# Graph stack of four layers: feature sums in column groups, spreads as one float32r pass, the diagonal as a row of the last row tile

## The chip, the cores and the metric

The kernel runs on one core of a Trainium2 chip. The metric is the device time of one execution in microseconds (us). Before the change the median of 14 runs is 944.88 us, from 942.43 to 948.26. Engines are called PE (TensorE, with PEld for its weight loads), DVE (VectorE), ACT (ScalarE), POOL (GpSimd) and SP (SyncE, which issues most DMAs).

## What is computed

The input is a feature matrix x of 2708 nodes by 128 features and a sparse, non-negative adjacency of 2708 x 2708, all float32. Four layers follow one another, each as x = layernorm(x + layer(x, adj)) without learned scale: graph convolution, an attention by degrees, a hyperbolic layer and a layer with node and edge weights. The last two and the norms, cut to what matters here:

```python
def _layernorm(x, axis=-1, eps=1e-5):
    m = jnp.mean(x, axis=axis, keepdims=True)
    v = jnp.var(x, axis=axis, keepdims=True)
    return (x - m) / jnp.sqrt(v + eps)

# layer 1: attention
H = A @ (att @ XW)
# layer 2: hyperbolic
h = proj(mobius_add(proj(mobius_matvec(weight, x)), proj(expmap0(bias))))
support_t = adj @ logmap0(h)
h = proj(expmap0(support_t))          # needs the norm of every node's row
xt = relu(logmap0(h))
h = proj(expmap0(xt))                 # and the norm after relu
# layer 3: node and edge
node_output = concat((adj > 0) @ x, (adj < 0) @ x) @ node_weight + node_bias * diag(adj)[:, None]
edge_output = (adj @ x) @ edge_weight + edge_bias * diag(adj)[:, None]
out = node_output + edge_output + x
```

## The kernel before

Nodes are cut into NT = 22 tiles of 128 rows (the last has 20) and into NB = 6 column blocks of 512 nodes (the last has 148). From the attention's end on, activations lie feature-major: 128 features on the partitions, the block's nodes along the free side. All of the change but its constants lies in `fast_rest` (from L1458), which runs from about 504 us to the end, in three stages of six blocks each.

*Attention stage.* `product(weights, b)` (L1486) sums 22 f32 matmuls over the adjacency's row tiles, taken from `pieces` (L1770), which loads two halves of a column block per call through SP (L1784, and L1789 for the 20-row tile). `after_attention(b)` (L1531) adds the old x (L1538), squares (L227), gets the variance of every node by `feature_sums` (L1502: per tile of 128 nodes one matmul with the squares as weights and one output column, so node-major), takes sqrt and reciprocal (L1541, L1542), spreads the result over the features with four transposes (`spread`, L241), multiplies (L1544) and makes `mx` (L1548). After blocks 2, 4 and 5 `hyperbolic` (L1562) works on the tiles so far, on DVE and ACT alone, and writes the h tiles (L1570).

*Hyperbolic stage.* The same product on h. `after_hyperbolic(b)` (L1646) needs two norms per node: sums of the squares of the product (usq) and of its relu (rsq), both by `column_sums_at` (su, L1502); then on 128 x 8 elements sqrt, reciprocal and Tanh (L1657 to L1664), a spread (pg), the residual (L1669), a mean by a 512-column matmul with a matrix of 1/128 (L1671), its subtraction (L1672), and `norm_wide` (L245): square, a 512-column matmul for the variance (L248), sqrt and reciprocal on 128 x 512 (L249, L250), and the multiply. The products with the last layer's weights (pp, L1677) give `edge` (L1685) and `node` as two float32r terms (L1688, L1689).

*Last stage.* For every row tile k there is an f32 matmul with `edge` (L1715) and two float32r ones of `node` with a 0/1 mask of the adjacency (L1704, L1724). Where k lies in the block, the diagonal comes in: `dg` is the adjacency tile times the identity on DVE (L1735), and a matmul with `bsum`, the sum of both biases in every row, adds it (L1736). Then the residual (L1745), `norm_wide` and the store (L1748).

A float32 matmul shows in the profile as two MATMUL records, a float32r one as one. PSUM work tiles come from `scratch()`, which goes round three tags and four buffers. The engines' instruction orders are set when the program is built, by a scheduler with pins in the source (`issue_after`, `queued`), and each engine runs its own in turn. Column groups of the PE array, where a matmul's output lies on 32 of the PSUM partitions or on one row at 0, 32, 64 or 96, occur once before: `whole_sum` (L758), for four row sums of the first attention steps.

## Time and profile before

| | us |
|---|---|
| median of 14 runs | 944.88 |
| the profiled execution | 945.75 |
| its span, first to last instruction | 944.0 |
| PE busy in the span | 883.2 |
| DVE busy | 538.6 |
| ACT busy | 368.2 |
| attention stage | 515 to 632 |
| hyperbolic stage | 654 to 763 (its product begins at 626) |
| last stage | 763 to 944 |
| mean granted PE clock | 0.965 |

The stages were read from the timeline of PE. A page's group row gives the line, the engine, output and inputs by name, the shapes and the count; after the bar come the busy time and the mean ns of one, then the idle time of the engine ahead of it and what released it. In the timeline a row starts with start and length in us, and brackets give the idle time ahead and the releaser. In a row by windows each engine's busy time stands with its number of instructions, then the granted clock, the DMA share and GB/s.

### The profile page before, as it was taken

To read this page: it belongs to the slowest core of one execution; us is meant where nothing else is said; L and a number is where in the kernel's file an instruction comes from. 1 tells how busy PE (TensorE), PEld (TensorE's weight loads), DVE (VectorE), ACT (ScalarE), POOL (GpSimd) and SP (SyncE) were. 2 spreads that over 40 slices of the span, in tenths; PEclk is the share of its full clock that TensorE was granted. 3 is DMA by queue.
4 is the path that set the end of the run, shared out by engine and by line. 5 is a ranking of instruction groups with operands and counts; after the bars stand their busy time and mean duration, and the time that the engine had idled before them with its cause. 6 is when DMAs were issued, how large, how long until landed. Compare 5 with 4: busy or idle time off the path is not lost.

```text
span 944.0 us, 9050 instructions
## 1 busy us (share of the span) xinstructions
PE 883.2 (94%) x3166; PEld 459.2 (49%) x3166; DVE 538.6 (57%) x1097; ACT 368.2 (39%) x595; POOL 149.0 (16%) x169
## 2 busy tenths in 40 slices
PE   3799999789799999999999999989999999999997
PEld 2344555435344444444444444454454555555555
DVE  4785557898588888887784004354423363444233
ACT  3776331210777776666663113355222221000000
POOL 5211000302765553222110000000000000000000
PEclk9799999797899999999999999999999999999998
DMA  9996930195596445334423677387664374555410
GB/s 342 369 317 231 301 120 23 50 386 201 189 351 213 148 154 168 118 123 143 148 88 121 242 262 267 118 322 271 236 228 156 100 291 163 197 180 200 148 44 15
DMA packets 93077, 182.81 MB, mean 194 GB/s; under 512 B 3680, under 2 KB 20784, under 8 KB 92896
## 3 DMA queue, kind: packets, MB, share of 16 engines
q1 hardware_dynamic: 82832, 142.35, 42.7%
q0 software_dynamic: 8320, 37.76, 12.1%
q10 hardware_dynamic: 1872, 2.04, 0.6%
q8 instruction: 27, 0.44, 0.2%
q14 instruction: 26, 0.21, 0.1%
HBM read 179.31 MB, written 2.83 MB: 193 GB/s over the span
## 4 chain that ended last, share of the span: by engine, by line
PE 80%; DVE 12%; DMA 4%; ACT 2%; issue 2%; ACTq 0%; DVEq 0%
PE a L1486 21%; PE uacc L1401 13%; PE a L1715 11%; PE a L821 10%; PE num L1436 7%; PE a L1724 6%; DVE att L1449 4%; DMA A<-in_adjT_dram 4%; PE t L758 2%; DVE jk L1203 2%; DVE att L1430 2%; PE var L248 1%; PE pp L1677 1%; PE su L1502 1%; PE low L1268 1%
## 5 line engine op out<-in xcount | busy, mean ns | idle before, releaser
L1401 PE MATMUL uacc<-att,xw_g 128*128 128x512 f32 (+1 forms) x312 | 130.4, 554 | 9.0 <-DVE att L1449 8.2
L1441 ACT ACTIVATE ln<-num,inval,occ_l 128x512 f32<-128x512 f32 (+1 forms) x156 | 106.5, 722 | 65.2 <-DVE gat L1440 62.8
L1715 PE MATMUL a<-cb,ut 128*128 128x512 f32 (+2 forms) x264 | 124.9, 555 | 0.0
L1724 PE MATMUL a<-mask,node 128*128 128x512 f32 (+2 forms) x264 | 123.0, 546 | 0.0
L1436 PE MATMUL num<-gat,w_all 128*128 128x512 f32 (+1 forms) x276 | 114.1, 543 | 0.0
L1486 PE MATMUL a<-cb,q_b 128*128 128x512 f32 (+2 forms) x264 | 108.4, 552 | 0.0
L821 PE MATMUL a<-A,q_b 128*128 128x512 f32 (+2 forms) x264 | 106.8, 552 | 0.7 <-DMA A<-in_adjT_dram 0.7
L1486 PE MATMUL a<-cb,xw 128*128 128x512 f32 (+2 forms) x264 | 106.1, 547 | 0.0
L1401 PEld LDWEIGHTS uacc<-att,xw_g 128*128 128x128 f32 x312 | 55.9, 189 | 90.7 <-issue 50.0
L1392 POOL DMA_INDIRECT gat<-in_adjT_dram,row_i x52 | 76.2, 1466 | 145.0 <-PE num L1436 77.4
L1440 DVE COPY gat<-num 2x512 f32<-2x512 f32 x150 | 85.8, 608 | 2.2 <-PE num L1436 2.0
L1449 DVE TENSOR_TENSOR att<-att,ln 128x1354 f32<-128x1354 f32 x52 | 81.1, 1560 | 9.8 <-ACT ln L1448 9.6
L1724 PEld LDWEIGHTS a<-mask,node 128*128 128x128 f32 (+1 forms) x264 | 49.0, 192 | 51.3 <-issue 50.7
L247 ACT ACTIVATE wsq<-s 128x512 f32<-128x512 f32 (+1 forms) x12 | 7.0, 581 | 169.8 <-DVE s L1745 137.0
L1436 PEld LDWEIGHTS num<-gat,w_all 128*128 128x128 f32 x276 | 51.2, 191 | 41.4 <-issue 22.7
L821 PEld LDWEIGHTS a<-A,q_b 128*128 128x128 f32 (+1 forms) x264 | 46.0, 191 | 50.3 <-issue 47.5
L1448 ACT ACTIVATE ln<-ln 128x1354 f32<-128x1354 f32 x52 | 69.4, 1334 | 1.3
L1430 DVE TENSOR_SCALAR att<-q_b,gj_l 128x1354 f32<-128x1354 f32 x52 | 48.0, 926 | 37.8 <-PE uacc L1401 37.8
L1486 PEld LDWEIGHTS a<-cb,q_b 128*128 128x128 f32 (+1 forms) x264 | 46.0, 191 | 48.1 <-issue 46.5
L1486 PEld LDWEIGHTS a<-cb,xw 128*128 128x128 f32 (+1 forms) x264 | 45.4, 190 | 47.2 <-issue 47.2
L1704 DVE TENSOR_SCALAR mask<-cb 128x3072 fp32r<-128x3072 f32 (+5 forms) x24 | 33.4, 1393 | 49.9 <-PE a L1724 49.9
L1036 ACT ACTIVATE xw<-A 128x2048 f32<-128x2048 f32 (+3 forms) x36 | 57.0, 1583 | 7.7 <-DMA A<-in_adjT_dram 6.8
(410 smaller groups left out, 937.5 us busy)
## 6 DMA issues: line engine op xcount, KB each, us to landing
cb<-in_adjT_dram SPq DMA_DIRECT2D x15, 2816.0 KB
cb<-in_adjT_dram SPq DMA_DIRECT2D x15, 2560.0 KB
A<-in_adjT_dram SPq DMA_DIRECT2D x25, 1024.0 KB
B<-in_adjT_dram SPq DMA_DIRECT2D x18, 1024.0 KB
cb<-in_adjT_dram SPq DMA_DIRECT2D x3, 814.0 KB
cb<-in_adjT_dram SPq DMA_DIRECT2D x3, 740.0 KB
ut<-in_adjT_dram SPq DMA_DIRECT2D x2, 1024.0 KB
A<-in_adjT_dram SPq DMA_DIRECT2D x5, 296.0 KB
```

The source lines that it names most:

```text
L821: nc.tensor.matmul(acc[c][:, :w], lhsT=z[:kw, k, :], rhs=t[:kw, i, :w], start=c not in begun, stop=(d == NB - 1 and k == NT - 1), skip_gro ...
L1392: return nc.gpsimd.indirect_dma_start(out=gat[g], out_offset=None, in_=adj_h, in_offset=bass.IndirectOffsetOnAxis(ap=row_i[:, h, g : g + 1 ...
L1401: nc.tensor.matmul(uacc[c][:, : cb - ca], lhsT=xw_g[:, g, :], rhs=att[:, ca:cb], start=(g == 0), stop=(g == GM - 1),)
L1430: nc.vector.tensor_scalar(att, q_b[:, h0 : h0 + HALF], gj_l[:, g : g + 1], 1.0, op0=ALU.mult, op1=ALU.max)
L1436: nc.tensor.matmul(num[:, : cb - ca], lhsT=(w_first if g < FIRST else w_all)[:, g, :], rhs=gat[g][:, ca:cb], start=True, stop=True)
L1440: nc.vector.tensor_copy(gat[g + 1][0:2, ca:cb], num[0:2, : cb - ca])
L1441: nc.scalar.activation(ln_n[:, ca:cb], num[:, : cb - ca], AF.Ln, scale=occ_l[:, g : g + 1], bias=inval[:, g : g + 1],)
L1448: nc.scalar.activation(ln_n, ln_n, AF.Exp, scale=-1.0)
L1449: nc.vector.tensor_mul(att, att, ln_n)
L1486: nc.tensor.matmul(acc[:, :w], lhsT=weights[:kw, k, :], rhs=pc[:kw, t, :w], start=(k == 0), stop=(k == NT - 1),)
L1715: nc.tensor.matmul(acc[:, :w], lhsT=edge[:kw, k, :], rhs=pc[:kw, t, :w], start=(k == 0), stop=False, skip_group_check=True,)
L1724: nc.tensor.matmul(acc[:, :w], lhsT=node[:kw, k, j, :], rhs=mask[:kw, t - ma, :w], start=False, stop=(k == NT - 1 and j == 1), skip_group_ ...
```

## The change

*Constants.* `sel` (128 x 4, float32r, made on POOL) has ones in rows 32i and 32i + 1 of column i. `odd` is 1 on odd partitions and `sign` 1 on even, -1 on odd ones (two DVE operations in `prepare_rest`).

*Feature sums.* `group_sums` takes the constant (ones or 1/128) as weights, 32 columns of it, and the squares of one tile of 128 nodes as the moving side; tile i's result goes to PSUM partitions 32i to 32i + 31. The sums of a block thus lie on four groups of partitions, 128 nodes along the free side. `group_spread` brings a value back over all features: ACT multiplies by `sign` and rounds to float32r, DVE adds the rest on the odd partitions, so even and odd rows add up to the value; then one float32r matmul per tile with a column of `sel` broadcast as weights. `group_roots` and `norm_groups` do sqrt, reciprocal and norm on 128 x 128 instead of 128 x 512.

*Where they are used.* Attention: blocks 0 to 4; the variances also go back to node-major by a matmul of 128 x 4 (`v4` with `ident[:, ::32]`), since `hyperbolic` needs them so. Block 5 keeps its form, but PE's order there is pinned: two, two and two row tiles of the next product stand before its st, pr and mx matmuls (`meanwhile`). Hyperbolic: all six blocks, with the mean as a third group sum of s and no mean matmul after the residual; the mean is subtracted ahead of the product with g. Last stage: blocks 0 to 4; block 5 keeps `norm_wide`.

*The diagonal.* `dg` and its matmuls go. The last row tile has 20 rows; its second-half piece gets the adjacency's diagonal of the block as row 20 (1 x 512, from `diag_d` in DRAM, through SP), and `edge` gets `bsum` as its row 20 (a DMA on POOL between the stages), so that the L1715 matmul of k = 21 adds the biases. `diag_d` is filled by one DMA of 2708 single elements on SP, right after `prepare_rest` and ahead of the loads of the attention's B tiles.

```diff
     nc.gpsimd.tensor_scalar(pad_big, pad_big, 1.0e30, None, op0=ALU.mult)
+    sel = const.tile([P, 4], F32R, tag="sel", name="sel")
+    sel_f = const.tile([P, 4], F32, tag="sel_f", name="sel_f")
+    nc.gpsimd.memset(sel_f, 0.0)
+    for i in range(4):
+        nc.gpsimd.memset(sel_f[32 * i : 32 * i + 2, i : i + 1], 1.0)
+    nc.gpsimd.tensor_copy(sel, sel_f)
+    odd = const.tile([P, 1], F32, tag="odd", name="odd")
+    sign = const.tile([P, 1], F32, tag="sign", name="sign")
     neg_sum = const.tile([P, NB * NB], F32, tag="neg_sum", name="neg_sum")
...
         nc.vector.tensor_add(bsum, b3n_s, b3e_s)
+        nc.vector.tensor_reduce(odd, ident.rearrange("p (a b) -> p b a", b=2)[:, 1, :], AX.X, ALU.add)
+        nc.vector.tensor_scalar(sign, odd, -2.0, 1.0, op0=ALU.mult, op1=ALU.add)
         centre(w3_s.rearrange("p (n f) -> p n f", f=F), 3, "w3_m")
...
     xw_d = tc.dram_tile([NP, F], F32, name="xw_d")
+    diag_d = tc.dram_tile([N, 1], F32, name="diag_d")
     w_col = w1ext[:, F : F + 1]
...
             prepare_rest()
+        nc.sync.dma_start(out=diag_d, in_=bass.AP(tensor=adjT.tensor, offset=0, ap=[[N + 1, N], [1, 1]]))
...
         rot = {"n": 0}
+        latest.clear()
...
-        def product(weights, b, name):
+        begun = {}
+        def product(weights, b, name, upto=NT, fixed=False):
             w = width(b)
-            acc = psum.tile([P, BW], F32, tag=f"acc{b % 3}", name=name)
-            for i in range(2):
-                pc = pieces(b, i)
-                for t in range(KH):
-                    k = i * KH + t
-                    kw = rows(k)
+            if name not in begun:
+                begun[name] = [psum.tile([P, BW], F32, tag=f"acc{b % 3}", name=name), 0, None]
+            acc, done, pc = begun[name]
+            for k in range(done, upto):
+                i, t = divmod(k, KH)
+                if t == 0:
+                    pc = pieces(b, i)
+                kw = rows(k)
+                with queued(PE) if fixed else nullcontext():
                     nc.tensor.matmul(
...
                     )
+            begun[name] = [acc, upto, pc]
             return acc
+        def meanwhile(b, n):
+            if b == NB - 1:
+                product(h, 0, "a2_0", n, True)
+                return queued(PE)
+            return nullcontext()
...
                 )
+        def group_sums(st, at, sq, b, w_cols):
+            for i in range(len(tiles(b))):
+                nc.tensor.matmul(
+                    st[32 * i : 32 * i + 32, at : at + P],
+                    lhsT=w_cols[:, :32],
+                    rhs=sq[:, i * P : (i + 1) * P],
+                    start=True,
+                    stop=True,
+                )
+        def group_spread(name, r, b):
+            n = len(tiles(b))
+            two = blk.tile([P, P], F32R, tag="two", name=f"two_{name}", bufs=3)
+            nc.scalar.activation(two[: 32 * n, :], r, AF.Copy, scale=sign[: 32 * n, :])
+            nc.vector.scalar_tensor_tensor(
+                two[: 32 * n, :], r, odd[: 32 * n, :], two[: 32 * n, :].bitcast(F32), op0=ALU.mult, op1=ALU.add
+            )
+            ps = scratch(name)
+            for i in range(n):
+                nc.tensor.matmul(
+                    ps[:, i * P : (i + 1) * P],
+                    lhsT=sel[: 32 * n, i : i + 1].to_broadcast([32 * n, P]),
+                    rhs=two[: 32 * n, :],
+                    start=True,
+                    stop=True,
+                )
+            return ps
+        def group_roots(name, st, b):
+            n = 32 * len(tiles(b))
+            r = blk.tile([P, P], F32, tag="gr", name=name)
+            nc.scalar.activation(r[:n, :], st[:n, :P], AF.Sqrt, bias=eps_c[:n, :])
+            nc.vector.reciprocal(r[:n, :], r[:n, :])
+            return r[:n, :]
+        def norm_groups(q, s, b, out):
+            st = scratch(f"st_{q}{b}")
+            group_sums(st, 0, square_block(s, b, f"sq_{q}{b}"), b, mean_w)
+            pr = group_spread(f"pr_{q}{b}", group_roots(f"gr_{q}{b}", st, b), b)
+            nc.vector.tensor_mul(out, s, pr[:, : width(b)])
...
             nc.vector.tensor_add(s[:, :w], acc[:, :w], x[:, cs])
-            st = feature_sums(square_block(s[:, :w], b, f"asq{b}"), b, f"st1_{b}", mean_w[:, 0:1])
+            asq = square_block(s[:, :w], b, f"asq{b}")
+            if b == NB - 1:
+                with meanwhile(b, 2):
+                    st = feature_sums(asq, b, f"st1_{b}", mean_w[:, 0:1])
+            else:
+                sg = scratch(f"sg{b}")
+                group_sums(sg, 0, asq, b, mean_w)
+                v4 = blk.tile([P, P], F32, tag="v4", name=f"v4_{b}")
+                nc.vector.tensor_copy(v4, sg[:, :P])
+                pr = group_spread(f"pr{b}", group_roots(f"gr{b}", sg, b), b)
+                st = scratch(f"st1_{b}")
+                nc.tensor.matmul(st[:, :4], lhsT=v4, rhs=ident[:, ::32], start=True, stop=True)
             nc.vector.tensor_copy(var[:, ta:tb], st[:, :n])
...
             nc.vector.reciprocal(rstd[:, ta:tb], rstd[:, ta:tb])
-            pr = spread(scratch(f"pr{b}"), rstd[:, ta:tb], b)
+            if b == NB - 1:
+                with meanwhile(b, 4):
+                    pr = spread(scratch(f"pr{b}"), rstd[:, ta:tb], b)
             nc.vector.tensor_mul(x[:, cs], s[:, :w], pr[:, :w])
...
                 pm = scratch(f"mx{t0}")
-                for i in range(2):
-                    nc.tensor.matmul(
-                        pm[:, i * (F + 1) : (i + 1) * (F + 1)],
-                        lhsT=x[:, (t0 + i) * P : (t0 + i + 1) * P],
-                        rhs=w2ext,
-                        start=True,
-                        stop=True,
-                    )
+                with meanwhile(b, 6):
+                    for i in range(2):
+                        nc.tensor.matmul(
+                            pm[:, i * (F + 1) : (i + 1) * (F + 1)],
+                            lhsT=x[:, (t0 + i) * P : (t0 + i + 1) * P],
+                            rhs=w2ext,
+                            start=True,
+                            stop=True,
+                        )
                 pv = pm[:, : 2 * (F + 1)].rearrange("p (t f) -> p t f", f=F + 1)
...
             s = blk.tile([P, BW], F32, tag="s", name=f"s2_{b}")
+            if w % P:
+                nc.gpsimd.memset(s[:, w : n * P], 0.0)
             su = scratch(f"su{b}")
-            column_sums_at(su, square_block(acc[:, :w], b, f"usq{b}"), b, ones[:, 0:1])
+            group_sums(su, 0, square_block(acc[:, :w], b, f"usq{b}"), b, ones)
             nc.vector.tensor_scalar(s[:, :w], acc[:, :w], 0.0, None, op0=ALU.max)
-            column_sums_at(su, square_block(s[:, :w], b, f"rsq{b}"), b, ones[:, 0:1], at=n)
-            nr = small("unr", 8)
-            inv = small("uinv", 8)
-            nc.vector.tensor_scalar(nr[:, : 2 * n], su[:, : 2 * n], MIN_NORM2, None, op0=ALU.max)
-            nc.scalar.activation(nr[:, : 2 * n], nr[:, : 2 * n], AF.Sqrt)
-            nc.vector.reciprocal(inv[:, : 2 * n], nr[:, : 2 * n])
-            g = small("g", 4)
-            nc.vector.tensor_scalar(g[:, :n], inv[:, :n], ATANH_MAX, 1.0, op0=ALU.mult, op1=ALU.min)
-            nc.vector.tensor_mul(g[:, :n], g[:, :n], nr[:, n : 2 * n])
-            nc.scalar.activation(g[:, :n], g[:, :n], AF.Tanh)
-            nc.vector.scalar_tensor_tensor(
-                g[:, :n], g[:, :n], MAXNORM, inv[:, n : 2 * n], op0=ALU.min, op1=ALU.mult
-            )
-            pg = spread(scratch(f"pg{b}"), g, b)
+            group_sums(su, 2 * P, s, b, mean_w)
+            group_sums(su, P, square_block(s[:, :w], b, f"rsq{b}"), b, ones)
+            pm = group_spread(f"mean{b}", su[: 32 * n, 2 * P : 3 * P], b)
+            nr = blk.tile([P, 2 * P], F32, tag="unr", name=f"unr{b}", bufs=1)[: 32 * n]
+            inv = blk.tile([P, 2 * P], F32, tag="uinv", name=f"uinv{b}", bufs=1)[: 32 * n]
+            g = blk.tile([P, P], F32, tag="ug", name=f"ug{b}", bufs=1)[: 32 * n]
+            nc.vector.tensor_scalar(nr, su[: 32 * n, : 2 * P], MIN_NORM2, None, op0=ALU.max)
+            nc.scalar.activation(nr, nr, AF.Sqrt)
+            nc.vector.reciprocal(inv, nr)
+            nc.vector.tensor_scalar(g, inv[:, :P], ATANH_MAX, 1.0, op0=ALU.mult, op1=ALU.min)
+            nc.vector.tensor_mul(g, g, nr[:, P:])
+            nc.scalar.activation(g, g, AF.Tanh)
+            nc.vector.scalar_tensor_tensor(g, g, MAXNORM, inv[:, P:], op0=ALU.min, op1=ALU.mult)
+            nc.vector.tensor_sub(s[:, :w], s[:, :w], pm[:, :w])
+            pg = group_spread(f"pg{b}", g, b)
             nc.vector.tensor_mul(s[:, :w], s[:, :w], pg[:, :w])
             nc.vector.tensor_add(s[:, :w], s[:, :w], x[:, cs])
-            pm = scratch(f"mean{b}")
-            nc.tensor.matmul(pm[:, :w], lhsT=mean_w, rhs=s[:, :w], start=True, stop=True)
-            nc.vector.tensor_sub(s[:, :w], s[:, :w], pm[:, :w])
-            norm_wide(scratch(f"var2_{b}"), s[:, :w], b, x[:, cs], blk.tile([P, BW], F32, tag="sq", name=f"wsq2_{b}"), blk.tile([P, BW], F32, tag="rs", name=f"rs2_{b}"))
+            norm_groups("l2_", s[:, :w], b, x[:, cs])
             for t0 in range(ta, tb, 2):
...
+        kw = rows(NT - 1)
+        nc.gpsimd.dma_start(out=edge[kw : kw + 1, NT - 1, :], in_=bsum[0:1, :])
...
             for i in range(2):
-                pc = pieces(b, i)
+                pc = pieces(b, i, i == 1)
                 for ma, mb in ((0, 6), (6, KH)):
...
                         kw = rows(k)
+                        ke = kw + (k == NT - 1)
                         nc.tensor.matmul(
                             acc[:, :w],
-                            lhsT=edge[:kw, k, :],
-                            rhs=pc[:kw, t, :w],
+                            lhsT=edge[:ke, k, :],
+                            rhs=pc[:ke, t, :w],
                             start=(k == 0),
...
                             )
-                        if k in tiles(b):
-                            o = k * P - b * BW
-                            dg = blk.tile([P, P], F32, tag="dg", name=f"dg{k}")
-                            nc.vector.tensor_mul(dg[:kw, :kw], pc[:kw, t, o : o + kw], ident[:kw, :kw])
-                            nc.tensor.matmul(
-                                acc[:, o : o + kw],
-                                lhsT=bsum[:kw, :],
-                                rhs=dg[:kw, :kw],
-                                start=False,
-                                stop=False,
-                                skip_group_check=True,
-                            )
             s = blk.tile([P, BW], F32, tag="s", name=f"s3_{b}")
...
             ob = blk.tile([P, BW], F32, tag="ob", name=f"ob{b}")
-            norm_wide(scratch(f"var3_{b}"), s[:, :w], b, ob[:, :w], blk.tile([P, BW], F32, tag="sq", name=f"wsq3_{b}"), blk.tile([P, BW], F32, tag="rs", name=f"rs3_{b}"))
+            if b == NB - 1:
+                norm_wide(scratch(f"var3_{b}"), s[:, :w], b, ob[:, :w], blk.tile([P, BW], F32, tag="sq", name=f"wsq3_{b}"), blk.tile([P, BW], F32, tag="rs", name=f"rs3_{b}"))
+            else:
+                norm_groups("l3_", s[:, :w], b, ob[:, :w])
             nc.sync.dma_start(out=outT[:, cs], in_=ob[:, :w])
...
-                def pieces(b, i):
+                def pieces(b, i, diagonal=False):
...
                     if i:
-                        nc.sync.dma_start(out=t[: rows(NT - 1), full, :w], in_=adjT[k0 + full * P :, cs])
+                        kw = rows(NT - 1)
+                        nc.sync.dma_start(out=t[:kw, full, :w], in_=adjT[k0 + full * P :, cs])
+                        if diagonal:
+                            nc.sync.dma_start(
+                                out=t[kw : kw + 1, full, :w], in_=diag_d[cs, :].rearrange("c o -> o c")
+                            )
                     return t
```

## The prediction

> **What bounds the kernel now.** I read the page from the top: busy shares, then the chain.
>
> ```profile
> span 944.0 us, 9050 instructions
> PE 883.2 (94%) x3166; PEld 459.2 (49%) x3166; DVE 538.6 (57%) x1097; ACT 368.2 (39%) x595; POOL 149.0 (16%) x169
> PE 80%; DVE 12%; DMA 4%; ACT 2%; issue 2%; ACTq 0%; DVEq 0%
> ```
>
> TensorE sets the end. The change lies in the three stages after 515 us, so I cut there (PE busy is the first figure after the length):
>
> ```profile
> 515.00:632.00 117.00, 114.22 (x369) 57.53 (x368) 30.13 (x152) 32.08 (x92) 0.19 (x1) 0.99 0.67 237
> 654.00:763.00 109.00, 106.88 (x357) 56.14 (x356) 38.58 (x62) 32.09 (x55) 0.19 (x1) 0.99 0.58 207
> 763.00:924.00 161.00, 161.00 (x520) 92.56 (x519) 64.07 (x76) 11.81 (x22) 0.21 (x1) 0.99 0.45 161
> ```
>
> PE never stops inside a stage. A PE pass added or removed there moves the end by its cadence, and DVE and ACT matter only where PE waits: at the two seams. The timeline of PE around them:
>
> ```profile
> 625.37 0.61 PE L1502 MATMUL st<-mean_w,asq 128*128 128x1 f32 x4 [0.96 <-ACT asq L227]
> 628.76 0.66 PE L241 MATMUL pr<-ident,rstd 128*128 128x128 f32 x2 [1.81 <-DVE rstd L1542]
> 758.49 1.13 PE L1671 MATMUL mean<-s,mean_w 128*128 128x512 f32 x2 [0.55 <-DVE s L1669]
> 761.12 1.99 PE L248 MATMUL var<-wsq,mean_w 128*128 128x512 f32 x2 [1.50 <-ACT wsq L247]
> ```
>
> Last, the groups that the change touches (window 500 to 944 us):
>
> ```profile
> L248 PE MATMUL var<-wsq,mean_w 128*128 128x512 f32 x20 | 12.4, 706 | 2.0 <-ACT wsq L247 1.9
> L1736 PE MATMUL a<-dg,bsum 128*128 128x128 f32 x42 | 8.1, 273 | 0.0
> L1671 PE MATMUL mean<-s,mean_w 128*128 128x512 f32 x10 | 5.5, 627 | 0.6 <-DVE s L1669 0.6
> L1502 PE MATMUL su<-ones,rsq 128*128 128x1 f32 x44 | 5.4, 242 | 0.0
> L241 PE MATMUL pg<-ident,g 128*128 128x128 f32 x22 | 3.4, 273 | 0.0
> ```
>
> These durations overlap, so I price by cadence (start to start). Two records make one f32 matmul: 512 columns cost 0.86 us, 0.92 with what stands around a lone one; four feature sums 0.79 to 0.85; a spread of four transposes 0.43 (0.108 each); an L1736 product 0.22 (a k step of the last stage takes 1.54 with it, 1.32 without).
>
> **The Trainium skill.** "TensorEngine Tiling (Array Packing)", Tiling Modes, says that tiles of the array work in parallel and that changing the mode drains the engine. The trace agrees: `whole_sum` (L758) already uses four column groups; at 196.28 its four 512-column f32 matmuls start 7 ns apart and end within 0.86 us, where in turn they would take 3.4. Entering the mode leaves 0.10 us, leaving it 0.15 to 0.2: 0.3 a visit. "TensorE: Matmul & The Clock Gate", Part 1, says that idle time lowers the clock; here, after the wait before 628.76, 512-column passes take 0.85 us instead of 0.43 for about two passes. "DMA: Bandwidth & Descriptors", on the semaphore increment of 16, lets a hardware-issued DMA use the largest k up to 16 that divides the outer dimension: 2708 = 4 x 677 gives 4 engines and 677 descriptors each. No transfer of before shows that count.
>
> **The change part by part.** One visit of `group_sums` (four 128-column f32 matmuls side by side) is 0.21 (a quarter of 0.86) plus 0.30 = 0.51; bounds 0.21 and, run in turn, 0.86 + 0.30. A spread by four one-pass f32r matmuls is shown nowhere. The L1724 f32r passes cost 0.23 at 512 columns, so 0.06 each if only streaming counts, 0.19 if each waits for its weight load (192 ns on the page). I take the transposes' 0.108, so 0.43; bounds 0.24 and 0.76.
>
> *Attention, five blocks:* sums 0.79 become 0.51; a 128 x 4 matmul on `ident` that brings the variances back to node-major adds 0.21; spread alike. −0.07 each, −0.4 in all. The q_b writes (0.61 us for two at L1570) come ahead of block 3's x: +0.5.
>
> *Hyperbolic, five blocks:* before: su 1.62, pg 0.43, mean 0.93, var 0.91 = 3.89. After: one visit for usq 0.51, a double one for s and rsq 0.72, one for the norm 0.51, three spreads 1.29 = 3.03. −0.86 each, −4.3; the short block 5 pays its mode changes, +0.5. Between su and pg now lie a 128 x 256 reciprocal (1.75 by 6.3 ns a column; 0.20 before), ACT and DVE steps and a table load (1.28): 6.3 to 6.9 us, under 7.3 to 8.2 us of PE work queued between. Hidden with 1.0 to 1.5 to spare in blocks 0 to 3; without that cover up to 0.5 a block.
>
> *Last stage:* 22 L1736 products go, −4.8; five var products go, −4.55; five visits plus spreads come, +4.7. Their st and pr waits beside mask work on DVE +0.4. Total −4.2. The DVE multiplies for L1736 also go, worth nothing (DVE 40% busy). Block 5's norm keeps its form, so the tail from 937.5 to 944 stays.
>
> *Seam attention to hyperbolic:* waits and slow clock cost 4.1 before (1.1 + 2.0 + 1.0). PE's order there is now written out: two k steps of the next product before st_5, two more before pr_5, two more before mx_5. But on ACT block 5's sqrt stands behind block 4's Ln and Tanh and their table loads (1.28 each); before, it came ahead of Tanh. Adding up: its reciprocal ends 8.5 us after the product's end, PE reaches pr_5 after 4.0. A wait of 4.6 plus 2.3 of slow clock, about 7: +3 (bounds 0 and +4). What is late next: x, mx_5 and the h tiles 20 and 21, needed about 30 us after the product's end and ready at 29. It takes part of the 0.5 margin that h had (ready 649.5, read 649.9).
>
> *Seam hyperbolic to last:* 4.6 before. After: no mean wait of 0.55, no var wait of 1.5 with its clock; instead pg waits 1.7 (chain 6.3 against 4.6 of PE work, no next product behind it), and the first mask on DVE holds up a spread by 0.6; 0.7 for mode changes and clock. 3.0: −1.5 (bounds −3 and +1).
>
> *DMAs.* The diagonal goes to `diag_d` on SP behind the A loads, ahead of the B loads (first B issue 99.7 us). At 9 ns of engine time a packet (what 8-byte packets on the ACT queue show) it takes 677 x 9 ns = 6 us; at the 86 ns apart that those show between 2-KB packets, 58. The B tiles land by 126 and are first used at 178.6 (L758): 52 us of cover, the DMA nearly idle from 126 on. I take it as hidden; at 58 it would cost about 6. On SP its issue stands ahead of the twenty B issues, which need nothing from it but their turn. The six 1 x 512 row loads follow 2.8-MB loads on the same queue, issued a block ahead; only the next load stands behind them. POOL has nothing else to do after 500 us, and its `edge` row has 28 us until k = 21 of block 0. I put all of these at nothing under that cover.
>
> Sum: −0.4 + 0.5 − 4.3 + 0.5 − 4.2 + 3 − 1.5 = −6.4. The profiled run took 945.75 against a median of 944.88, so it is 0.9 above; the difference is applied to the median: 938.5. (1.75 of it lie outside the span, and I leave them as they are.)
>
> **The rivals.**
> *A, more than summed:* a mode change costs 0.1 instead of 0.3 a visit, and the written k steps cover half of what the first seam gains: about 25 visits x −0.2 = −5, and −1.5, so −12.9: 932. For it: L758's 7 ns; against it: the drains seen beside it.
> *B, the seam eats it:* pr_5's wait drags mx_5 past the h tiles' use; 5 to 6 instead of 3, and hyperbolic pg waits in blocks 0 to 3 cost 0.5 each: 942.5. For it: Ln and Tanh ahead in ACT's order; against: h still arrives within a microsecond of its use.
> *C, slower: f32r spreads bound by their weight loads.* Each of about 106 new f32r matmuls then costs 0.19 to 0.22 instead of 0.108, +0.08 to 0.11 each, +9 to +12: 949. It decides from 0.17 us a matmul on, where 106 x 0.06 eats the 6.4. For it: the LDWEIGHTS of 192 ns stand beside every f32r pass, and here no 0.43 us f32 pass hides them. Against: the transposes have loads of the same 128 columns (0.12 to 0.14 each) and keep 0.108.
> *D, slower too: diagonal descriptors at 90 ns or more*, 61 us, 9 beyond the cover; the B loads wait behind it on the same engines, and L758 at 178.6 for them: 938.5 + 9 = 947.5, and more if slower still.
> *E, no change in effect:* column groups in turn, 0.64 x 25 visits = +16, is excluded by L758 unless 128-column passes behave otherwise; I give it 0.02 within C's side.
>
> **How the numbers follow.** Main case 0.50 (934.5 to 941.5), A 0.14, B 0.16, C with E 0.12, D 0.08. Predicted: 938.5. Range: A's 931 to 947: C and D's 0.2 lies mostly above, their milder half within. The measurement tells about 0.2%, 1.9 us, from no change: faster takes the main case, A and half of B, 0.50 + 0.14 + 0.08 = 0.72; same takes the other half of B: 0.08; slower C and D, 0.20.
>
> **What the profile of the changed kernel would show.** L1736 gone and k steps of the last stage all 1.32 apart. The four matmuls of `group_sums` starting within 20 ns, with 0.1 us ahead of them and 0.2 behind. The four f32r matmuls of a spread 0.43 us from first to last end; 0.7 or more means C. PE waiting some 4 to 5 us ahead of pr_5, released by DVE's rstd. After the hyperbolic stage one wait near 1.7 on DVE's or ACT's part of `two_pg`, and none for mean or var. Windows before 515 us unchanged; a wait of L758 on a B tile means D. Wrong altogether if PE shows idle time inside a stage, which before had none.

## The result and the profile after

The changed kernel takes 939.56 us (median of 10 runs, 936.55 to 941.62) beside 944.59 for the one before: 0.9947 of it, 95% interval 0.9935 to 0.9958. A second measurement of the same kernel, beside the last experiments, gave 0.9955 (0.9940 to 0.9971). So it is some 5 us faster; 938.5 was forecast. The sum is right to about 1.4 us, but two of its terms, those of the seams, were wrong by more, with opposite signs.

The page after begins:

```profile
span 935.7 us, 9403 instructions
PE 871.7 (93%) x3290; PEld 447.0 (48%) x3290; DVE 536.8 (57%) x1115; ACT 380.5 (41%) x629; POOL 150.1 (16%) x178
```

The span fell by 8.3 us, more than the medians. That is chance ahead of the change: the first product of the attention stage starts at 508.77 us before and at 504.73 after, on code that is the same but for the diagonal's load and the constants. Over all traces of this study that start lies between 504.7 and 511.4 (509.51 in a second trace of the very same changed kernel), with PE's clock low in different places. From that start on, the stages of one program repeat closely: 430.96 and 430.84 us in the two traces of the changed kernel, 435.26 before. So I compare traces from there. "Slow clock" and "slow passes" below mean stretches in which the profile shows PE's granted clock at half.

The windows of both kernels, cut at the same points of the program (the end of the attention products, of block 1's and block 4's hyperbolic product, of blocks 1, 4 and 5 of the last stage; each row gives the length, the busy time of PE, PEld, DVE, ACT and POOL, PE's granted clock, the DMA share, GB/s). Before:

```profile
515.20:624.10 108.90, 108.90 (x352) 54.41 (x351) 24.76 (x115) 27.03 (x84) 0.19 (x1) 1.00 0.64 226
624.10:672.00 47.90, 45.12 (x124) 21.01 (x123) 26.89 (x158) 23.81 (x44) 0.00 (x0) 0.96 0.81 294
672.00:749.10 77.10, 77.04 (x237) 38.87 (x236) 26.26 (x41) 21.63 (x40) 0.00 (x0) 1.00 0.48 165
749.10:828.60 79.50, 77.45 (x287) 47.51 (x286) 33.47 (x49) 12.87 (x24) 0.40 (x2) 0.98 0.59 213
828.60:922.40 93.80, 93.80 (x296) 53.11 (x295) 35.42 (x36) 3.96 (x6) 0.00 (x0) 1.00 0.41 144
922.40:937.10 14.70, 14.31 (x93) 12.39 (x92) 6.16 (x7) 1.32 (x2) 0.00 (x0) 0.88 0.05 19
```

After:

```profile
511.00:619.00 108.00, 108.00 (x364) 52.18 (x362) 30.74 (x127) 29.05 (x87) 0.19 (x1) 1.00 0.65 228
619.00:664.50 45.50, 42.15 (x139) 18.82 (x139) 27.91 (x161) 26.59 (x53) 0.00 (x0) 1.00 0.84 306
664.50:739.70 75.20, 75.20 (x301) 36.35 (x300) 29.27 (x53) 26.05 (x52) 0.19 (x1) 1.00 0.51 173
739.70:821.70 82.00, 78.81 (x310) 45.49 (x309) 32.48 (x46) 15.58 (x31) 1.12 (x4) 0.96 0.57 207
821.70:913.30 91.60, 91.60 (x301) 50.88 (x300) 26.31 (x27) 4.22 (x9) 0.00 (x0) 1.00 0.44 148
913.30:929.40 16.10, 15.70 (x102) 14.64 (x101) 4.44 (x8) 1.40 (x3) 0.00 (x0) 0.79 0.05 18
```

Where nothing waits, the change gives about what was forecast: rows three and five are 1.9 and 2.2 us shorter. Row four, the seam from the hyperbolic to the last stage, is 2.5 longer, with PE idle for 3.2 us and the clock at 0.96; the last row is 1.4 longer at a clock of 0.79. The timeline of PE after, around both seams and behind block 4's last norm:

```profile
620.87 1.98 PE L1506 MATMUL a<-cb,q_b 128*128 128x512 f32 x4 [1.60 <-DMA cb<-in_adjT_dram]
626.77 0.40 PE L250 MATMUL pr<-ident,rstd 128*128 128x128 f32 x2 [1.75 <-DVE t L1660]
...
749.49 0.63 PE L1557 MATMUL pg<-two_pg,sel 128*128 128x128 f32 x4 [1.16 <-DVE two_pg L1552]
751.45 1.18 PE L1810 MATMUL a<-cb,ut 128*128 128x512 f32 x2 [1.33 <-DMA cb<-in_adjT_dram]
753.25 1.22 PE L1819 MATMUL a<-mask,node 128*128 128x512 f32 x2 [0.62 <-DVE mask L1798]
754.26 1.91 PE L1810 MATMUL a<-cb,ut 128*128 128x512 f32 x2
...
915.88 0.43 PE L1538 MATMUL st_l<-sq_l,mean_w 128*32 128x128 f32 x8 [0.40 <-ACT sq_l L236]
916.23 0.86 PE L1810 MATMUL a<-cb,ut 128*128 128x148 f32 x2
```

At both seams PE now waits for `cb`, the first load of the next stage; the prediction had named no such wait. At the second seam three waits follow one another, and the pair of L1810 passes takes 1.91 us instead of 1.02, until 759.3: the slow clock. Behind 915.88 the short block's pairs take 0.79 instead of 0.46 until 923. Rows by windows, cut where the clock changes, show half the clock for 6.8 us at both places:

```profile
752.40:759.20 6.80, 6.18 (x11) 3.39 (x11) 3.70 (x5) 2.10 (x3) 0.00 (x0) 0.50 1.05 378
916.20:923.00 6.80, 6.80 (x33) 6.77 (x30) 2.62 (x4) 0.77 (x2) 0.00 (x0) 0.50 0.11 40
```

So each of them can have cost at most 3.4 us.

### The profile page after: what moved, and what is told of

It reads as the page before. It is cut to its first block, busy times and chain, and to the rows that moved or that the text cites. A ratio compares the mean times of both kernels' runs of the same rounds, so it can differ in the third digit from the quotient of the medians.

```text
span 935.7 us, 9403 instructions
## 1 busy us (share of the span) xinstructions
PE 871.7 (93%) x3290; PEld 447.0 (48%) x3290; DVE 536.8 (57%) x1115; ACT 380.5 (41%) x629; POOL 150.1 (16%) x178
## 4 chain that ended last, share of the span: by engine, by line
PE 79%; DVE 13%; DMA 5%; issue 2%; ACT 1%; ACTq 0%; DVEq 0%
PE a L1506 21%; PE uacc L1414 13%; PE a L1810 11%; PE a L833 10%; PE num L1449 7%; PE a L1819 6%; DVE att L1462 5%; DMA A<-in_adjT_dram 4%; DVE att L1443 2%; DVE jk L1216 2%; PE t L770 2%; DMA cb<-in_adjT_dram 1%; PE pp L1768 1%; PE low L1281 1%; PE xw L981 1%
## 5 line engine op out<-in xcount | busy, mean ns | idle before, releaser
L1810 PE MATMUL a<-cb,ut 128*128 128x512 f32 (+2 forms) x264 | 127.5, 566 | 1.3 <-DMA cb<-in_adjT_dram 1.3
L236 ACT ACTIVATE sq_l<-s 128x512 f32<-128x512 f32 (+1 forms) x11 | 6.6, 604 | 136.5 <-DVE s L1828 110.0
```

What stands on the lines that cost most here:

```text
L1810: nc.tensor.matmul(acc[:, :w], lhsT=edge[:ke, k, :], rhs=pc[:ke, t, :w], start=(k == 0), stop=False, skip_group_check=True,)
```

## The experiments

Stages in us from the traces (start of the attention products to their end; to the end of hyperbolic block 1; of block 4; of block 1 of the last stage; of block 4; of block 5; the rest; every cut lies at the start of the last pass of an adjacency product), and the medians as ratios to runs of the kernel before on the same chip:

| kernel | attention | seam 1 | hyp. 2-4 | seam 2 | last 2-4 | block 5 | rest | sum | ratio (95%) |
|---|---|---|---|---|---|---|---|---|---|
| before | 115.36 | 47.86 | 77.15 | 79.47 | 93.77 | 14.76 | 6.88 | 435.26 | 1 |
| changed | 114.26 | 45.54 | 75.18 | 81.98 | 91.63 | 16.05 | 6.32 | 430.96 | 0.9947 (0.9935-0.9958) |
| changed, again | 114.26 | 45.53 | 75.18 | 81.85 | 91.64 | 16.07 | 6.32 | 430.84 | 0.9955 (0.9940-0.9971) |
| diagonal alone | 115.36 | 46.50 | 77.15 | 77.60 | 91.00 | 13.21 | 6.32 | 427.13 | 0.9920 (0.9894-0.9946) |
| without diagonal | 114.26 | 45.53 | 75.19 | 81.85 | 94.21 | 14.09 | 6.89 | 432.02 | 0.9978 (0.9962-0.9994) |
| last norms wide | 114.25 | 45.53 | 75.18 | 81.39 | 91.28 | 13.22 | 6.32 | 427.18 | 0.9900 (0.9873-0.9926) |
| split 24 | 114.26 | 45.53 | 75.18 | 75.51 | 91.64 | 17.63 | 6.75 | 426.51 | 0.9884 (0.9856-0.9911) |
| split 24, wide | 114.26 | 45.53 | 75.19 | 74.91 | 91.28 | 13.21 | 6.75 | 421.12 | 0.9852 (0.9823-0.9880) |
| split 24, wide in 4, 5 | 114.26 | 45.53 | 75.19 | 75.56 | 91.64 | 13.21 | 6.74 | 422.13 | 0.9874 (0.9833-0.9916) |
| before, split 24 | 115.37 | 46.50 | 77.15 | 76.39 | 93.77 | 13.47 | 6.83 | 429.48 | 0.9965 (0.9947-0.9983) |
| split 12 | 114.26 | 46.81 | 75.16 | 80.11 | 91.64 | 13.83 | 6.74 | 428.55 | 0.9939 (0.9919-0.9959) |
| split 12, more pins | 114.26 | 47.47 | 75.18 | 80.00 | 91.64 | 13.83 | 6.75 | 429.14 | 0.9947 (0.9931-0.9962) |
| all three | 114.26 | 47.47 | 75.18 | 75.03 | 91.28 | 13.22 | 6.70 | 423.15 | 0.9889 (0.9862-0.9915) |
| all, spans | 112.78 | 53.84 | 73.07 | 74.85 | 90.84 | 13.20 | 6.68 | 425.25 | 0.9908 (0.9872-0.9943) |

**The load at the second seam.** The theory was that it sets the seam: it needs the buffer of block 4's second half, and in the trace of the changed kernel it is issued at 740.33, 0.6 us after the last pass of block 4 starts, and lands at about 751.4. The edit cuts it in two:

```diff
-                    nc.sync.dma_start(
-                        out=t[:, :full, :w],
-                        in_=adjT[k0 : k0 + full * P, cs].rearrange("(t p) c -> p t c", p=P),
-                    )
+                    for ca, cb in ((0, 6), (6, full)) if n in (24,) else ((0, full),):
+                        nc.sync.dma_start(
+                            out=t[:, ca:cb, :w],
+                            in_=adjT[k0 + ca * P : k0 + cb * P, cs].rearrange("(t p) c -> p t c", p=P),
+                        )
```

> The changed kernel, with the first load of the last stage (11 row tiles) cut into two DMAs, tiles 0 to 5 and 6 to 10. Theory LOAD: the seam from the hyperbolic to the last stage is set by this load, which can go out only when block 4's product has given its buffer free and lands 11 us later; the waits of 1.33 (load) and 0.62 us (mask, which reads the same load) and about 4 us of slow clock behind them are its price. The first six tiles then land about 4 us sooner, both waits and most of the slow clock go: 935 to 936.5 us, 3 to 4.5 below the changed kernel's 939.6. Theory CHAIN: the seam is set by the chain of ACT and DVE to two_pg and the wait of 1.16 us on it, and the load only comes last by chance: within 1 us of 939.6.

Measured: 933.79 us, 0.9884, some 6 us under the changed kernel, more than the theory said. Theory CHAIN, as it was put, is out. The PE timeline of this run:

```profile
752.59 1.12 PE L1810 MATMUL a<-cb,ut 128*128 128x512 f32 x2
754.15 1.02 PE L1810 MATMUL a<-cb,ut 128*128 128x512 f32 x2
...
757.81 0.64 PE L1557 MATMUL pg<-two_pg,sel 128*128 128x128 f32 x4
```

No wait and no slow clock is left at this seam, and it falls from 81.98 to 75.51: 3.1 of the 6.5 us are the three waits. But the scheduler also put pg behind four edge products (L1810) of the last stage, which the early tiles make possible: the wait for two_pg is hidden by them. Load and chain were in the way together; the load left PE nothing to do while the chain ran. How much the cut gives without the new order wasn't tried.

The control on the kernel before, with the same edit:

> The kernel before, with the first load of the last stage cut in two as in the changed kernel's run. There the load lands about 760.7 us and PE comes to it at 762.9, after its waits for mean and variance: theory LOAD says that it is covered, so nothing is gained except what the scheduler's new order brings: within 1.5 us of before. If cutting the load helps by itself (fewer bytes ahead of the first matmul, whatever the change): 4 to 5 us faster, as in the changed kernel.

Measured: 940.15, 0.9965 (0.9947 to 0.9983), 3 us faster; the seam shrinks from 79.47 to 76.39. The expectation was wrong: I had the load as covered, since it lands before PE comes. Its timeline shows what it missed:

```profile
755.45 1.12 PE L1715 MATMUL a<-cb,ut 128*128 128x512 f32 x2
756.41 1.02 PE L1671 MATMUL mean<-s,mean_w 128*128 128x512 f32 x2
757.74 0.74 PE L1724 MATMUL a<-mask,node 128*128 128x512 f32 x2 [0.31 <-DVE mask L1704]
```

The first row tile of the last stage now fills the waits for mean and var. A load that lands before it is asked for may still forbid the order that would fill a wait. Here too a stretch of slow clock, 3.4 us long behind the var wait of before, is gone. Yet the seam gains 6.5 us after the change and 3.1 before, so about half of the gain belongs to what the change laid bare.

**The diagonal alone, and the change without it.** The first is the kernel before with the change's hunks for `diag_d`, `edge` and `pieces` only. The second takes these hunks out of the changed kernel again and puts the old lines back:

```diff
-                        ke = kw + (k == NT - 1)
+                        ke = kw
...
+                        if k in tiles(b):
+                            o = k * P - b * BW
+                            dg = blk.tile([P, P], F32, tag="dg", name=f"dg{k}")
+                            nc.vector.tensor_mul(dg[:kw, :kw], pc[:kw, t, o : o + kw], ident[:kw, :kw])
...
```

> The kernel before with the diagonal as a row of the last row tile, and nothing else of the change. If each L1736 product costs its cadence of 0.22 us, 22 of them give -4.8: 939.8 us, about as much as the whole change; the seam keeps its spare time ahead of the load, so nothing is given back. Rival: the gain of the change is mostly that of the hyperbolic stage's sums, and the products with the diagonal are partly hidden: 942 us or more.

> The changed kernel with the products of the diagonal put back as they were (22 DVE multiplies, 22 matmuls), without the DMAs of the diagonal. By the traces the group sums and spreads save about 5.5 us up to the end of the hyperbolic stage and lose as much at the seam and in the last block's slow clock: 944 us (943 to 945), as before. Rival, all parts keep what they save: 940 us.

Measured: 937.31 us, 0.9920, and 941.53 us, 0.9978. The diagonal by itself brings more than the whole change; the sums and spreads by themselves bring 2 us, less than the rival and more than the theory. Blocks 2 to 4 give the price of an L1736 product cleanly: 93.77 to 91.00 is 2.77 for 12, 0.23 each, so 5.1 for 22 (predicted 4.8). The rest of the diagonal's measured 7.5 stands in the trace as slow clock that isn't there this time (seam 1, block 5); the interval reaches from 5.1 to 10, so it can't be told from 5.1. Together they don't add up: by the traces the two parts gain 8.1 and 3.2 us, the whole change 4.3. Half of the 7.1 us between lies in block 5, which is slow with the whole change and with neither part (3.5). At seam 2 it is 2.0: taking the diagonal's products away gives 1.87 in the old kernel (79.47 to 77.60) and nothing in the new one (81.85 to 81.98), where the load sets the time. And 1.4 is the slow clock of before at seam 1, which both parts count as theirs.

**Wide norms in the last stage.**

```diff
-            if b == NB - 1:
+            if True:
                 norm_wide(scratch(f"var3_{b}"), s[:, :w], b, ob[:, :w], blk.tile([P, BW], F32, tag="sq", name=f"wsq3_{b}"), blk.tile([P, BW], F32, tag="rs", name=f"rs3_{b}"))
```

> The changed kernel with the old wide norm (one 512-column matmul for the variance, reciprocal on 128 x 512) in all six blocks of the last stage. From the trace a group sum with its spread costs 1.07 us of PE there, the wide product 0.92, so -0.15 a block, and block 4 has one place less where PE changes mode or waits ahead of the short last block, whose k steps ran at the slow clock for 7 us: -0.7 to -2.5, so 937 to 939 us. Rival, that the sums in groups pay in this stage too as the prediction had it (0.94 against 0.91, and shorter chains): the same within 0.7 or slower, 939.6 to 941.

Measured: 935.26 us, 0.9900, 4 us under the changed kernel and past the expected range. Blocks 2 to 4 gain 0.12 each, as said. The larger part is block 5: 16.05 to 13.22. To tell whether it is all blocks or block 4's norm, two more runs, both with the split load, the second with `if b >= NB - 2:` in that place:

> The changed kernel with the split load of the last stage and the wide norm in all blocks of the last stage. The two gains lie in different places (the seam; the norms of blocks 0 to 4 and the slow clock behind block 4's), so they should add up: about 5 + 3.6 below the changed kernel, 930 to 931 us, and no slow clock behind 751 us or in the last block. If the wide norm's gain was itself the luck of the clock, 933.

> Split load of the last stage, and the wide norm in blocks 4 and 5 of the last stage only; blocks 0 to 3 keep the groups. If the wide norm's gain of about 3 us (930.6 against 933.7) is the slow clock behind block 4's norm, this keeps nearly all of it: 931 to 931.5, 0.1 us a block for the other four. If it is the sums and spreads of every block: 933.

Measured: 930.56 (0.9852) and 933.18 (0.9874). The first adds up, and is the fastest kernel of the study: 1.5% under before. The second's interval covers both expectations; its trace says 422.13 us for the changed stages against 421.12 with all norms wide and 426.51 with the groups, so block 4's norm is most of it. Both forms wait 0.40 us there; in these runs only behind the groups do the passes slow down. The wide one, in the first run of this part:

```profile
919.72 1.13 PE L257 MATMUL var<-wsq,mean_w 128*128 128x512 f32 x2 [0.40 <-ACT wsq L256]
920.68 0.41 PE L1810 MATMUL a<-cb,ut 128*128 128x148 f32 x2
```

Yet in three traces with the groups (13.83 twice, and 14.09 with the diagonal's products put back) block 5 has no slow passes, but a second wait, of 0.9 us on two_pr_l, that the slow passes otherwise cover:

```profile
L1557 PE MATMUL pr_l<-two_pr_l,sel 128*128 128x128 f32 x4 | 0.6, 280 | 0.9 <-DVE two_pr_l L1552 0.9
```

That is the row of the run "split 12". And the first trace of before has slow passes with the wide form. In all 14 traces PE waits 0.39 to 0.40 us at this norm; half the clock follows in three of six with the groups (6.8, 6.8 and 10.2 us of it) and in one of eight with the wide form (3.4). So the groups cost about 0.6 here in any case (13.83 against 13.21); what decides on the other 2 to 4 us stays open.

**The first seam.** The same cut with `n in (12,)`, alone, and then with

```diff
-                with meanwhile(b, 4):
+                with meanwhile(b, 8):
...
-                with meanwhile(b, 6):
+                with meanwhile(b, 10):
```

> The changed kernel with only the first load of the hyperbolic stage cut in two (tiles 0 to 5, 6 to 10). At the first seam PE waits 1.76 us for this load and, five instructions on, 1.92 us for pr_5, whose reciprocal ends at a time that the load does not set. Theory CHAIN at this seam: the first wait goes, the second grows to about 3.7, nothing gained: within 1 us of the changed kernel. Theory LOAD: the load sets this seam too: 1.5 to 2 us faster.

> As the run before, and PE's written order has six instead of two row tiles of the next product between st_5 and pr_5 (two, eight and ten in all before st, pr and mx instead of two, four and six). If both the load and the chain to pr_5 are covered by work that has to be done anyway, both waits go: 3 to 3.7 us faster than the changed kernel. If h's tiles or the second half load then come too late, the gain is below 1.5.

Measured: 939.31 (0.9939) and 939.75 (0.9947): nothing gained, seam 1 even longer (46.81 and 47.47 against 45.54). Both waits do go, and a new one comes, at k = 12 of the next product, with 3.4 us of slow clock behind it in both traces; here of each run the wait of PE:

```profile
634.00 1.97 PE L1506 MATMUL a<-cb,q_b 128*128 128x512 f32 x2 [2.72 <-DVE q_b L1660]
```

```profile
635.72 2.07 PE L1506 MATMUL a<-cb,q_b 128*128 128x512 f32 x2 [3.23 <-DVE q_b L1660]
```

It is h tile 12, written by the hyperbolic step of block 4; its write ends 0.05 us ahead of each of these passes. In the changed kernel it is written 13.6 us after the attention products' end and read 1.8 later. In these two runs it is written after 14.6 and 15.1, so little of the 1.8 was left to gain. That is neither of the two theories: the chain that sets this seam ends further on than pr_5. Two more runs: "all three" joins both cuts, these pins and the wide norms; "all, spans" has both cuts and the wide norms, with the old pins and

```diff
-        spans = {2: (0, 12), 4: (12, 20), 5: (20, 22)}
+        spans = {2: (0, 12), 3: (12, 16), 4: (16, 20), 5: (20, 22)}
```

> Both first loads split, six more row tiles written ahead of pr_5, and the wide norm in the whole last stage: the gains of all, 5 + 3.6 + 3.5 below the changed kernel: 926 to 928 us, with PE waiting at neither seam for more than 0.5 us. If the scheduler's new order in the hyperbolic stage puts waits elsewhere: 929 to 931.

> Both first loads split, wide norms in the last stage, and the hyperbolic step for tiles 12 to 15 made after attention block 3 instead of with block 4. Theory H12: with the load out of the way the first seam is set by h tile 12, which the chain of block 4 delivers 13.6 us after the end of the attention products, so that PE waits about 3 us at the twelfth row tile; an earlier tile 12 moves the wait to tile 16, needed 3.4 us later: 2 to 3 us below the best run so far (930.6), 928. If DVE's and ACT's added work in block 4 delays its norm: 930 to 932.

Measured: 934.43 (0.9889) and 937.22 (0.9908). The first is slower than without the edits at seam 1, by the same wait of 3.23 us and one of 1.58 on h tile 20. The second is worse still:

```profile
645.56 2.07 PE L1506 MATMUL a<-cb,q_b 128*128 128x512 f32 x2 [4.56 <-DVE q_b L1660]
```

Tile 12 is now written at 621.71, before the attention products end, and the wait has moved to tile 16, as theory H12 had it. But tile 16 is written only at 645.51, 21.4 us after the products' end, where "all three" has it after 18.3, and seam 1 takes 53.84. ACT makes seven table loads of 1.28 us between 630 and 643 on the way there; how much of the delay is theirs wasn't separated. That h sets this seam once the load is away is shown by four traces; that an earlier tile 12 would shorten it is not.

**The changed kernel again.**

> The changed kernel itself, beside these on one chip: 0.9935 to 0.996 of before. If the slow clock of 8 us behind the seam's waits belongs to the program's waits, the trace has it again at the same place (first product of the last stage, 751 to 760 us); that behind block 4's last norm may come or not.

Measured: 0.9955. The seam's waits recur, and the slow passes with them (half the clock for 6.8 us again):

```profile
754.26 0.63 PE L1557 MATMUL pg<-two_pg,sel 128*128 128x128 f32 x4 [1.16 <-DVE two_pg L1552]
755.97 1.12 PE L1810 MATMUL a<-cb,ut 128*128 128x512 f32 x2 [1.08 <-DMA cb<-in_adjT_dram]
757.77 1.22 PE L1819 MATMUL a<-mask,node 128*128 128x512 f32 x2 [0.67 <-DVE mask L1798]
758.78 1.91 PE L1810 MATMUL a<-cb,ut 128*128 128x512 f32 x2
```

Block 5 is slow again too, 16.07. The four other traces of changed kernels with this load uncut have waits on two_pg and on the load too, and half the clock with them, for 6.8 us in two and for 3.4 in two.

## Why the prediction was right, and where it was not

The table's stages by the prediction's own terms, in us:

| stretch | predicted | measured |
|---|---|---|
| attention products | +0.1 | -1.1 |
| seam 1 with hyperbolic blocks 0, 1 | +2.1 (seam +3, sums -0.9) | -2.3 |
| hyperbolic 2 to 4 | -2.6 | -2.0 |
| seam 2 with blocks 0, 1 of the last stage | -3.5 (diagonal -1.8, sums and waits of the blocks -0.2, seam -1.5) | +2.5 |
| last stage 2 to 4 | -2.3 | -2.1 |
| block 5 and the rest | -0.3 | +0.7 |
| sum | -6.5 | -4.3 |

That the sum came out is luck in part: the first seam and the attention products gave 5.6 us more than forecast, the second seam and block 5 7.0 less, and these errors lie in different terms with different causes.

*Attention products: better than forecast.* The 0.5 for the q_b writes did not come (PE is busy 108.00 of 108.00), and the five blocks give about 0.2 each instead of 0.07.

*Prices of the new operations: right.* The groups run side by side and the f32r spreads are not bound by their weight loads:

```profile
741.18 0.43 PE L1538 MATMUL su<-usq,ones 128*32 128x128 f32 x8
741.53 0.77 PE L1506 MATMUL a<-cb,q_b 128*128 128x148 f32 x4
...
744.41 0.66 PE L1557 MATMUL mean<-two_mean,sel 128*128 128x128 f32 x4
744.90 3.43 PE L1506 MATMUL a<-cb,q_b 128*128 128x148 f32 x24
```

A visit takes 0.35 from its first start to the next product, with about 0.1 ahead of it (predicted 0.51 in all); a spread 0.49 from its first start to the next product, of which about 0.1 is still the pass before it (predicted 0.43; rival C needed more than 0.68). Rivals C and E are out. So is A: a visit is 0.24 above the estimated 0.21 of its streaming, not 0.1, and 932 lies below every run of the changed kernel. B, too: pr_5's wait is 1.75 instead of 5 to 6, and hyperbolic blocks 2 to 4 have no idle time (75.20 of 75.20).

*Hyperbolic blocks: size off.* -0.66 a block instead of -0.86.

*Seam attention to hyperbolic: a failed step.* "Its reciprocal ends 8.5 us after the product's end, PE reaches pr_5 after 4.0" had two errors. PE starts the next product only when its load lands, after a wait of 1.60, so it reached pr_5 5.7 us after the product's end at 619.3; and the reciprocal ended at 626.6, 7.3 after it. The order on ACT was as forecast, block 5's sqrt behind the table loads of block 4's step. The wait was 1.75 and drew no slow clock, where I had 4.6 and 2.3. The prediction also looked for h tiles 20 and 21 as next late; with the load cut, the runs show that tile 12 is. About 1.35 of the 2.3 gained is slow clock in the first trace of before, which two other traces with the same code there do not have (46.50).

*Seam hyperbolic to last: the other failed step,* -1.5 predicted. The wait on two_pg was right in kind (1.7 predicted, 1.16), but the load's 1.33 was not in the sum. The mask's 0.62 follows from it, and only its size agrees with the 0.6 of the prediction: no mask holds up a spread, but DVE starts on the mask when the load lands, and PE waits for its end. The slow clock, up to 3.4 us, was put at 0.7 together with the mode changes. With the load cut, the stretch comes to 75.51, 4.0 under before, near the -3.5 that the sum has for it. But that agreement is luck again: the same cut takes the kernel before to 76.39. With the load cut in both, the change gains 0.9 there; eight products of the diagonal are 1.8 of it, so the sums and spreads of this stretch (hyperbolic blocks 4 and 5, block 0 of the last stage) cost about 0.9 more than what they replace, where the sum had 0.2 less. That is an estimate by subtraction; which of the three blocks it is stays open.

*Block 5: not foreseen.* The waits of st and pr were put at 0.4 for all blocks together. In this trace block 5 takes 2.8 us more behind the groups than behind the wide form (16.05 against 13.22); about 0.6 of it is the groups' own, the rest slow clock.

*The diagonal's DMA: hidden, as forecast.* SP issues it at 98.18:

```profile
98.18 0.76 SPq L1092 DMA_DIRECT2D diag_d<-in_adjT_dram  x1
```

The 4-byte packets run from 99 to 113 us, 14 us, between the bounds of 6 and 58; by the trace's packet records one takes 22 ns on average and four run at a time, the four engines of the prediction at more than twice its 9 ns. It does hold SP up: the second B load is issued at 113.01, where it was at 100.15 before. But the B tiles are used from 177 us on, and the whole-sum line (L770) waits for none. Rival D is out.

## What to carry to other kernels

At a seam between stages, list what must have arrived before PE can start the next stage: the load of its first operand (freed buffer + 11 us here), the chain that makes its other operand, and the norm in between; removing work ahead of them only moves PE to the latest of these. A large first load can be cut so that the first row tiles land early, and that gives the scheduler work with which to fill other waits. And price a wait together with the slow clock that may come with it: 3.1 us of waits came with half the clock for 6.8 us, up to 3.4 us more.

## What the runs showed of the hardware

PE was granted half its clock for 6.8 us amid waits of 1.16, 1.33 and 0.62 us within 5 us, and again at the same place of the program in the second trace of the changed kernel (1.16, 1.08 and 0.67). Behind a single wait of 0.39 to 0.40 us, half the clock came in four traces (3.4, 6.8, 6.8 and 10.2 us) and not in ten others. Even behind the same wait of 3.23 us on h tile 12 it came in one run ("split 12, more pins", 3.4 us) and not in another ("all three"), so a wait's length alone does not tell. From 500 us to the end of the last products every stretch of half clock in the 14 traces lasts 3.4 us or two or three times that. 2708 single 4-byte elements in one DMA took 14 us. Four 128-column f32 matmuls on four column groups cost 0.45 us a visit, though streaming alone would take 0.21, an estimate from the 0.86 of a 512-column one.
